# Layer 0's experts add their rows to the tokens in memory; layer 1's thresholds, casts and order of work change engines and places

## The chip, the cores and the metric

The kernel runs on one core of one Trainium2 chip, in one launch. The core has a matrix engine (TensorE, PE in the profile), a vector engine (VectorE, DVE), an engine for activations and copies (ScalarE, ACT), a general one (GpSimd, POOL) and one that only issues transfers (SyncE, SP). Each engine works through its own list of instructions in order; semaphores tie the lists together. Indirect transfers (gathers and scatters by a list of row numbers) are issued by POOL, plain ones mostly by SP. The metric is the time of the launch on the device in microseconds; 2173.75 is the median of three runs before the change.

## The reference

Two transformer layers work on 4096 tokens (2 sequences of 2048) of 256 numbers in float32. In both, attention and experts run beside each other on the normed tokens:

```
xn = layernorm(x)
x = x + attention0(xn) + experts0(xn)
xn = layernorm(x)
x = x + attention1(xn) + experts1(xn)
```

- `attention0`: causal attention with 16 heads, queries through a rank of 64, keys and values through a rank of 32, rotary positions, softmax.
- `experts0`: softmax over 8 experts, the best two per token; token and choice get a place in the expert's buffer while it has room (1280 places). An expert computes `(gelu(x Wa) * (x Wg)) Wout` with 512 hidden numbers. The two results of a token are weighed by its gates and summed.
- `attention1`: each token attends to 32 learned patterns per head by *sparsemax*: the 32 scores are sorted, summed up, and a threshold `tau` is found, so that `max(z - tau, 0)` sums to one.
- `experts1`: sigmoid scores, the best two of 8 experts per token; each expert's weight is the mean gate of its tokens; `down(silu(gate x) * (up x))` with 128 hidden numbers; and a shared expert with 256 hidden numbers for all tokens.

## The kernel before, in words

**Layer 0.** Attention fills the first 1200 us; a planner written by hand gives small jobs due times (`later("S", ISSUE, due, job)` puts a transfer on SP from a due time on). Its results, residual and attention, are stored to `x1` in memory (`store_sum`). The router and the dispatch run inside it: each normed token row is scattered to its expert's place in `buf` (line 654), with two more numbers, the row to which the result is to go and the gate (`ROW` is 258). `clear` (line 635) has filled `buf` beforehand; an empty place has 1e6 as the row to go to. `clear` also fills the result buffer `oe` of 2 x 4096 rows, by 16 transfers of 512 KB.

The experts follow (lines 1281 to 1296). An expert has 1152 places, in three steps of 384. Rows are turned by TensorE (L1252) and copied to `inT` by ScalarE and VectorE (L1254, L1256); for each of four parts of the hidden numbers TensorE makes `pa` and `pg` (L1265, two buffers each), ScalarE the gelu `ge` (L1267), VectorE the product `hT` (L1268); then TensorE makes `py` for three tiles of 128 rows (L1272), VectorE weighs them into `ys` (L1275) and POOL scatters `ys` to `oe` (L1276), choice 0 in the first half, choice 1 in the second, so that every row is written at most once. Rows with 1e6 are beyond `bounds_check` and are not written. Four views of `oe` that are declared disjoint (`out_ways`) let up to four scatters be under way. The numbers `to` and `gates` are cast and copied from the rows by VectorE (L1241, L1243), two buffers each.

**Layer 1.** Here all work is a list of tasks with an engine, a guessed duration, a lag, what they come after, and buffers (`Plan`, lines 49 to 127). `Plan.write` merges them: at each point it takes the earliest task, and on its engine, among those that could start about then, the one of the lowest rank (`RANKS`, line 1389, by function name), then the one with the longest way to the end. It thus writes one fixed order for each engine before anything runs; every instruction so written has line 138 in the profile.

- `prepare` (line 1446), for eight groups of 512 tokens: `add_results` (line 1425) loads the two `oe` halves and adds them to `x_sb` (which the expert loop has loaded from `x1`); mean and variance per tile (`bn_stats`, `bn_aggr`); `roots` makes the inverse root by 13 small instructions on VectorE; ScalarE norms into `xn`; TensorE turns (`tp`), ScalarE copies to `xT`, TensorE makes the router's logits (`po`), `bias_` adds on VectorE.
- `shared`: the shared expert's products (`gu`, `acc`). `router`: sigmoid, best two, counts, places. `dispatch`: 64 scatters of `xn` rows to `buf1`, from POOL.
- `routed`, 20 blocks of 512 places: POOL gathers the expert's weights from `wall`, SP loads the rows, VectorE casts the row numbers `to` (`places`), TensorE, ScalarE and VectorE compute, POOL scatters to `oe`.
- `sparsemax` (line 1775), 8 batches: VectorE and ScalarE sort by compares (tile `srt`), VectorE scans, finds `tau`; POOL subtracts it (`less`, `z<-z,tau`). `attend` and `project` use the result. All this needs only `xT`, and fills the time of dispatch and routed blocks.
- `combine` adds the two `oe` halves to `x_sb`; `store` writes the output.

Of the kernel before, what the change touches and what calls it, by code (L numbers as in the profile page):

```python
# [11 lines left out]
F32 = mybir.dt.float32  # L12
# [10 lines left out]
NT = B * S  # L23
# [25 lines left out]
class Plan:  # L49
# [3 lines left out]
    class Task:  # L53
        __slots__ = ("eng", "ns", "f", "after", "new", "lag", "nr", "rank", "way", "left", "ready", "next", "end", "at")
# [16 lines left out]
    def add(self, eng, ns, f, after=(), new=(), use=(), lag=0, rank=0):  # L71
        t = Plan.Task()
        t.eng, t.ns, t.f, t.after, t.new, t.lag, t.rank = eng, ns, f, list(after), list(new), lag, rank
        t.next, t.end, t.way = [], None, 0
        for h in list(new) + list(use):
            h.users.append(t)
        self.tasks.append(t)
        return t

    def write(self, until=0, slow=1):  # L80
# [27 lines left out]
        while ready:  # L108
# [4 lines left out]
            s, t = max((z for z in cand if z[1].eng == t0.eng and z[0] <= (soon if z[1].rank < t0.rank else s0 + near)), key=lambda z: (-z[1].rank, z[1].way))  # L113
# [32 lines left out]
def moe_transformer_kernel(  # L146
# [15 lines left out]
    x1 = dram.tile([NT, E], F32, name="x1")  # L162
# [111 lines left out]
    with ExitStack() as actx:  # L274
# [15 lines left out]
        zero = attw.tile([P, ROW], F32, name="zero")  # L290
# [30 lines left out]
        G.iota(number, pattern=[[NT, 2], [P, NTILE]], base=0, channel_multiplier=1)  # L321
# [235 lines left out]
        def store_sum(bq):  # L557
            sdma(x1.rearrange("(t p) d -> p t d", p=P)[:, 4 * bq:4 * bq + 4], xos[bq])
# [76 lines left out]
        def clear(b, i):  # L635
            n = b.shape[1]
            sdma(b[512 * i:512 * i + 512].rearrange("(p a) d -> p a d", a=4), bc(zero[:, 0:n], 1, [P, 4, n]))
# [501 lines left out]
        pin(G.memset(zero[:, E:ROW], 1e6))  # L1139
# [4 lines left out]
        later("S", 9 * ISSUE, 40000, load_out_weights, None, 2)  # L1144
        for i in range(NSLOT // 512):
            later("S", ISSUE, 50000 + 12000 * i, lambda i=i: clear(buf, i), None, 2)
            later("S", ISSUE, 340000 + 40000 * i, lambda i=i: clear(buf1, i), None, 2)
            if i < 2 * NT // 512:
                later("S", ISSUE, 360000 + 40000 * i, lambda i=i: clear(oe, i), None, 2)
# [78 lines left out]
    with tc.tile_pool(name="moe", bufs=2) as mp, tc.tile_pool(name="moeh", bufs=3) as hp, \  # L1228
            tc.tile_pool(name="moetp", bufs=2, space=PSUM) as mtp, \
            tc.tile_pool(name="moeps", bufs=2, space=PSUM) as mps:  # L1230
        out_ways = bass_types.dram_disjoint_views(oe[:], 4)
# [26 lines left out]
        def feed_forward(wi, wt, inT, n, to, gates_e, c0):  # L1258
# [10 lines left out]
            for i in range(n // P):  # L1269
                py = mps.tile([P, E], F32, tag="py", name="py")  # L1270
                for f in range(4):
# [4 lines left out]
                G.indirect_dma_start(out_ways[c % 4], bass.IndirectOffsetOnAxis(ap=to[:, c:c + 1], axis=0), ys, None,  # L1276
                                     bounds_check=2 * NT - 1, oob_is_err=False)
# [3 lines left out]
        for e in range(NE):  # L1281
# [10 lines left out]
            SP.dma_start(x_sb[:, 4 * e:4 * e + 4], x1.rearrange("(t p) d -> p t d", p=P)[:, 4 * e:4 * e + 4])  # L1292
# [22 lines left out]
    SP.dma_start(fg_sb, fg[:, :, NE:NE + 2])  # L1315
    SP.dma_start(fu_sb, fu[:, :, NE:NE + 2])
    SP.dma_start(fd_sb, fd[:, NE:NE + 2])
    xT = l1x.tile([P, 2, NT], F32, name="xT")
    scale = l1x.tile([P, NTILE, NE], F32, name="scale")
    with tc.tile_pool(name="l1a", bufs=2) as lp, \  # L1320
# [5 lines left out]
        NZ = 3  # L1326
        head = lc.tile([P, H1, NPAT], F32, name="head")
# [54 lines left out]
        for i in range(4):  # L1382
# [7 lines left out]
            "add_results.take": 8, "attend.flip": 3, "attend.keep_": -1, "attend.weigh": 3, "prepare.flip": -4,  # L1390
            "prepare.keep_": -3, "prepare.logits": -2, "routed.down": 1, "routed.fetch": 3, "routed.flip": -1,
            "routed.hidden": 1, "routed.keep_": 2, "routed.out_": 2, "routed.places": 4, "router.slots": 4,
            "router.totals": -2, "scores.go": 3, "scores.keep_": -2, "shared.<lambda>": -2, "shared.down": 3,
            "sparsemax.<lambda>": 4, "sparsemax.copy": -1, "sparsemax.divide": 4, "sparsemax.largest": 6,
            "sparsemax.less": 3, "sparsemax.threshold": 5
# [17 lines left out]
        def results(src, k, grp, dst):  # L1413
# [5 lines left out]
        land0 = [zbuf[1 + i // 2].rearrange("p h i s -> p (h i s)")[:, 1024 * (i % 2):1024 * (i % 2) + 1024].rearrange(  # L1419
            "p (c e) -> p c e", c=4) for i in range(4)]  # L1420
        land1 = [xn_flat[:, 1024 * i:1024 * i + 1024].rearrange("p (c e) -> p c e", c=4) for i in range(8)]
        r_land = plan.ring(4), plan.ring(8)
        turn_land = cycle(land0), cycle(land1)

        def add_results(src, which_, grp, after, xn4=None):
# [3 lines left out]
            for k in range(2):  # L1429
                hold, st = plan.hold(r_land[which_]), {}  # L1430
                direct = k == 0 and xn4 is not None

                def load(k=k, st=st, direct=direct):
                    st["at"] = xn4 if direct else next(turn_land[which_])
                    results(src, k, grp, st["at"])

                def take(st=st):
                    pV.tensor_tensor(xs, xs, st["at"], ALU.add)
                d = add("S", 1700, load, after, new=[] if direct else [hold], lag=3500)
                last = [add("V", 1220, take, [d] + last, use=[] if direct else [hold])]  # L1440
# [3 lines left out]
        normed, turned, logged, added = {}, {}, [], []  # L1444

        def prepare(grp):
            mv = lc.tile([P, 4, 2], F32, name=f"mv{grp}")
            sm = lc.tile([P, 4, 4], F32, name=f"sm{grp}")
            rstd, v, t, nmr = (sm[:, i] for i in range(4))
            xn4 = xn[:, 4 * grp:4 * grp + 4, 0:E]  # L1450
            stats = []
            added.extend(add_results(oe, 0, grp, [], xn4))
            for i in range(4):
# [571 lines left out]
```

## Time and profile before

| what | us |
|---|---|
| median of three runs (2168.76 to 2175.24) | 2173.75 |
| the profiled execution | 2170.47 |
| its span in the profile | 2168.7 |
| layer 0, attention with router and dispatch | 0 to about 1206 |
| layer 0, experts | about 1206 to 1603 |
| layer 1, first normed tokens to last logits | 1617 to 1687 |
| layer 1, first scatter of the dispatch | 1706.7 |
| layer 1, rows of the first routed block asked for | 1813.7 |
| layer 1, last threshold | 2119 |

The profile is of one execution. A group's line gives the line of code, engine, operation, what it writes and reads, shapes and count; then its busy time and the mean of one in ns; then the engine's idle time ahead of it and what ended most of that. A line of the timeline gives start, duration, engine, line and operation, and in brackets the idle time before it with the one that ended it. "PEld" is a weight load of TensorE. The granted clock is a share of TensorE's full clock. Over the whole span TensorE is busy 89%, VectorE 65%; from 1603 on it is 440 and 474 of 566 us.

### The profile page before, as it was taken

To read this page: it belongs to the slowest core of one execution; us is meant where nothing else is said; L and a number is where in the kernel's file an instruction comes from. 1 tells how busy PE (TensorE), PEld (TensorE's weight loads), DVE (VectorE), ACT (ScalarE), POOL (GpSimd) and SP (SyncE) were. 2 spreads that over 40 slices of the span, in tenths; PEclk is the share of its full clock that TensorE was granted. 3 is DMA by queue.
4 is the path that set the end of the run, shared out by engine and by line. 5 is a ranking of instruction groups with operands and counts; after the bars stand their busy time and mean duration, and the time that the engine had idled before them with its cause. 6 is when DMAs were issued, how large, how long until landed. Compare 5 with 4: busy or idle time off the path is not lost. (4 is left out here: it accounts for less than half of the span.)

```text
span 2168.7 us, 26456 instructions
## 1 busy us (share of the span) xinstructions
PE 1927.2 (89%) x9497; PEld 1074.1 (50%) x9510; DVE 1408.9 (65%) x2010; ACT 912.6 (42%) x1815; POOL 696.2 (32%) x920
## 2 busy tenths in 40 slices
PE   4689998999999999999998899999977985788886
PEld 2344443444444444444443566666746653566664
DVE  4476788677775678777771222222248797999875
ACT  3044455355566555655667111111114232554442
POOL 4232212343335234231001111111210486365652
PEclk8599899899999999999999899999995998999999
DMA  5433311442324333141100712221032123334427
GB/s 155 126 99 101 109 60 38 123 121 96 94 63 138 102 106 99 58 120 53 37 11 11 249 42 85 91 92 49 25 116 70 44 83 112 92 115 123 128 101 232
DMA packets 151064, 204.45 MB, mean 94 GB/s; under 512 B 16393, under 2 KB 116881, under 8 KB 150930
## 3 DMA queue, kind: packets, MB, share of 16 engines
q1 hardware_dynamic: 131264, 151.55, 23.1%
q0 software_dynamic: 16640, 49.41, 6.6%
q10 hardware_dynamic: 3026, 1.77, 0.3%
q8 instruction: 76, 1.25, 0.2%
q14 instruction: 58, 0.48, 0.1%
HBM read 109.13 MB, written 98.79 MB: 96 GB/s over the span
## 5 line engine op out<-in xcount | busy, mean ns | idle before, releaser
L509 ACT ACTIVATE es<-sc 128x512 f32<-128x512 f32 (+3 forms) x1280 | 599.5, 535 | 457.6 <-PE sc L309 443.7
L470 DVE TENSOR_REDUCE part<-s 128x2 f32<-128x1024 f32 (+3 forms) x640 | 650.1, 1058 | 207.2 <-PE s L309 206.1
L309 PE MATMUL sc<-q,ks 128*128 128x512 f32 (+3 forms) x1280 | 426.4, 419 | 19.9 <-ACT es L509 19.5
L309 PEld LDWEIGHTS sc<-q,ks 128*128 128x128 f32 x1280 | 212.5, 192 | 248.3 <-ACT es L509 173.7
L309 PE MATMUL av<-es,va 128*32 128x512 f32 (+3 forms) x2560 | 300.9, 548 | 3.7 <-POOL es L511 2.1
L309 PE MATMUL s<-ks,q 64*128 64x512 f32 (+3 forms) x1280 | 253.0, 447 | 32.8 <-DVE part L470 10.9
L511 POOL TENSOR_SCALAR_AFFINE_SELECT es<-es 128x256 f32<-128x256 f32 x256 | 103.3, 407 | 555.8 <-ACT es L509 554.8
L138 DVE TENSOR_TENSOR srt<-srt 128x1024 f32<-128x1024 f32 (+3 forms) x224 | 231.7, 1072 | 7.0 <-ACT srt L138 0.2
L309 PEld LDWEIGHTS s<-ks,q 64*128 64x128 f32 x1280 | 111.7, 189 | 199.3 <-DVE part L470 113.3
L1276 POOL DMA_INDIRECT oe<-ys,to x72 | 70.0, 972 | 335.1 <-DVE ys L1275 330.2
L1268 DVE TENSOR_TENSOR hT<-ge,pg 128x384 f32<-128x384 f32 x96 | 53.1, 554 | 185.9 <-PE pg L1265 184.7
L1267 ACT ACTIVATE ge<-pa 128x384 f32<-128x384 f32 x96 | 47.1, 490 | 269.2 <-PE pa L1265 269.1
L138 POOL DMA_INDIRECT oe<-xn,to x80 | 100.3, 1254 | 101.4 <-ACT xn L138 82.8
L138 POOL DMA_INDIRECT buf<-xn,slot x64 | 86.1, 1345 | 118.1 <-DVE rc L138 98.9
L1265 PE MATMUL pa<-inT,wi 128*128 128x384 f32 x336 | 123.3, 486 | 0.0
L1265 PE MATMUL pg<-inT,wi 128*128 128x384 f32 x336 | 122.1, 486 | 0.0
L138 ACT COPY srt<-srt 128x1024 f32<-128x1024 f32 (+2 forms) x80 | 66.7, 834 | 120.9 <-DVE srt L138 120.1
L1272 PE MATMUL py<-wt,hT 128*128 128x256 f32 x504 | 112.2, 379 | 0.0
L309 PEld LDWEIGHTS av<-es,va 128*32 128x32 f32 x2560 | 55.6, 109 | 99.7 <-issue 75.9
L1272 PEld LDWEIGHTS py<-wt,hT 128*128 128x128 f32 x504 | 95.8, 190 | 17.5
L1275 DVE TENSOR_SCALAR ys<-py,gates 128x256 f32<-128x256 f32 x72 | 34.8, 484 | 86.2 <-PE py L1272 86.2
L1265 PEld LDWEIGHTS pg<-inT,wi 128*128 128x128 f32 x336 | 63.3, 190 | 42.7
(262 smaller groups left out, 2349.4 us busy)
## 6 DMA issues: line engine op xcount, KB each, us to landing
q<-qd SPq DMA_DIRECT2D x64, 256.0 KB
xn<-oe SPq DMA_DIRECT2D x24, 512.0 KB
buf<-zero SPq DMA_DIRECT2D x20, 516.0 KB
buf<-zero SPq DMA_DIRECT2D x20, 514.0 KB
xn<-buf SPq DMA_DIRECT2D x20, 514.0 KB
rows<-buf SPq DMA_DIRECT2D x8, 1161.0 KB
qd<-hi SPq DMA_DIRECT2D x16, 512.0 KB
qd<-lo SPq DMA_DIRECT2D x16, 512.0 KB
```

The costliest lines, as they stand in the source:

```text
L138: return lambda *a, **k: self.tc.keep_in_program_order(f(*a, **k))
L309: pin(PE.matmul(*args, **kw))
L470: pin(V.tensor_reduce(parts[j][:, i, 2 * pair:2 * pair + 2, kb], sc[:, :, :n], AX.X, ALU.max))
L509: pin(A.activation(es[:, g % 2, :n], sc[:, :n], AF.Exp, scale=0.25))
L511: pin(G.affine_select(es[:, :, 0:P], es[:, :, 0:P], pattern=[[0, 2], [1, P]], compare_op=ALU.is_ge, fill=0.0, base=0, channel_multiplier=-1))
L1265: PE.matmul(ps[:, :n], lhsT=wi[:, dc, col:col + P], rhs=inT[:, dc], start=dc == 0, stop=dc == 1)
L1267: A.activation(ge[:, :n], pa[:, :n], AF.Gelu)
L1268: V.tensor_tensor(hT[:, f, :n], ge[:, :n], pg[:, :n], ALU.mult)
L1272: PE.matmul(py, lhsT=hT[:, f, P * i:P * i + P], rhs=wt[:, f], start=f == 0, stop=f == 3)
L1275: V.tensor_scalar(ys, py, gates_e[:, c:c + 1], None, ALU.mult)
L1276: G.indirect_dma_start(out_ways[c % 4], bass.IndirectOffsetOnAxis(ap=to[:, c:c + 1], axis=0), ys, None, bounds_check=2 * NT - 1, oob_is_er ...
```

## The change

1. Layer 0's experts scatter `ys` to `x1` itself, with an addition in the transfer (`compute_op=ALU.add`), without bounds check and without disjoint views, so that each such scatter waits for the one before it. `x1` has 128 rows more; an empty place now has row 4096 (`NT`), the first of these, as the row to go to. The row numbers lose the half of `oe` (`NT*k`); layer 1's `mark` adds it.
2. The 16 clears of `oe` go; one small store clears the spare rows of `x1`, one writes the first 128 rows of `oe`. The layout of a clear is `(a p)` in place of `(p a)`.
3. In layer 1 `x_sb` is loaded from `x1` by eight transfers in `measure`, after the last scatter; the 16 loads of `oe` halves and the 16 additions go. The shared expert's weights are loaded behind the first of the eight. `roots` works on groups 0, 1, 2-3, 4-5, 6-7: five batches in place of eight.
4. `warm`: 12 products of 128 x 512 on TensorE, whose result nobody reads, ahead of the first transposes.
5. `less` moves from POOL to VectorE, the cast `places` of the routed blocks from VectorE to ScalarE.
6. New `RANKS`; a key `sub` that breaks ties of rank (the loads in order of groups); the first compares of the two halves of a batch one after the other; `plan.write`'s factor on TensorE's guessed durations before 60 us is 1.15 and not 1.8. In the order so written, most of the shared expert's products stand behind the router.

The diff, cut to its core ("..." marks what is left out; the new `RANKS` are in the full kernel, and `roots` has the same instructions as before on wider slices):

```diff
-            s, t = max((z for z in cand if z[1].eng == t0.eng and z[0] <= (soon if z[1].rank < t0.rank else s0 + near)), key=lambda z: (-z[1].rank, z[1].way))
+            s, t = max((z for z in cand if z[1].eng == t0.eng and z[0] <= (soon if z[1].rank < t0.rank else s0 + near)), key=lambda z: (-z[1].rank, -z[1].sub, z[1].way))
...
-    x1 = dram.tile([NT, E], F32, name="x1")
+    x1 = dram.tile([NT + P, E], F32, name="x1")
...
-        zero = attw.tile([P, ROW], F32, name="zero")
+        zero = attw.tile([P, E + 1], F32, name="zero")
+        zero0 = attw.tile([P, ROW], F32, name="zero0")
...
-        G.iota(number, pattern=[[NT, 2], [P, NTILE]], base=0, channel_multiplier=1)
+        G.iota(number, pattern=[[0, 2], [P, NTILE]], base=0, channel_multiplier=1)
...
         def clear(b, i):
-            n = b.shape[1]
-            sdma(b[512 * i:512 * i + 512].rearrange("(p a) d -> p a d", a=4), bc(zero[:, 0:n], 1, [P, 4, n]))
+            z, n = (zero0, ROW) if b is buf else (zero, E + 1)
+            sdma(b[512 * i:512 * i + 512].rearrange("(a p) d -> p a d", a=4), bc(z, 1, [P, 4, n]))
...
-        pin(G.memset(zero[:, E:ROW], 1e6))
+        pin(G.memset(zero[:, E:E + 1], 1e6))
+        pin(G.memset(zero0, 0.0))
+        pin(G.tensor_scalar(zero0[:, E:E + 1], meta[:, 0, 0, 0:1], float(NT), None, ALU.add))
...
+        later("S", ISSUE, 48000, lambda: sdma(x1[NT:NT + P], zero0[:, 0:E]), None, 2)
+        later("S", ISSUE, 49000, lambda: sdma(oe[0:P], zero[:, 0:E]), None, 2)
         for i in range(NSLOT // 512):
             later("S", ISSUE, 50000 + 12000 * i, lambda i=i: clear(buf, i), None, 2)
             later("S", ISSUE, 340000 + 40000 * i, lambda i=i: clear(buf1, i), None, 2)
-            if i < 2 * NT // 512:
-                later("S", ISSUE, 360000 + 40000 * i, lambda i=i: clear(oe, i), None, 2)
...
-        out_ways = bass_types.dram_disjoint_views(oe[:], 4)
...
                 V.tensor_scalar(ys, py, gates_e[:, c:c + 1], None, ALU.mult)
-                G.indirect_dma_start(out_ways[c % 4], bass.IndirectOffsetOnAxis(ap=to[:, c:c + 1], axis=0), ys, None,
-                                     bounds_check=2 * NT - 1, oob_is_err=False)
+
+                G.indirect_dma_start(x1[:], bass.IndirectOffsetOnAxis(ap=to[:, c:c + 1], axis=0), ys, None,
+                                     compute_op=ALU.add)
...
-            SP.dma_start(x_sb[:, 4 * e:4 * e + 4], x1.rearrange("(t p) d -> p t d", p=P)[:, 4 * e:4 * e + 4])
...
-    SP.dma_start(fg_sb, fg[:, :, NE:NE + 2])
-    SP.dma_start(fu_sb, fu[:, :, NE:NE + 2])
-    SP.dma_start(fd_sb, fd[:, NE:NE + 2])
...
+        WARM = 12
...
+        def shared_weights():
+            pS.dma_start(fg_sb, fg[:, :, NE:NE + 2])
+            pS.dma_start(fu_sb, fu[:, :, NE:NE + 2])
+            pS.dma_start(fd_sb, fd[:, NE:NE + 2])
...
-            added.extend(add_results(oe, 0, grp, [], xn4))
...
-            roots_ = add("V", 2200, roots, stats)
...
+        def roots(g0, g1):
...
+        def measure(grp):
+            def load():
+                pS.dma_start(x_sb[:, 4 * grp:4 * grp + 4],
+                             x1[512 * grp:512 * grp + 512].rearrange("(c p) d -> p c d", p=P))
+            d = add("S", 1700, load, lag=3500, sub=2 * grp)
...
+        def warm():
+
+            hold, st, last = plan.hold(r_pz), {}, []
+
+            def product():
+                if not st:
+                    st["pz"] = psum("pz")
+                pPE.matmul(st["pz"], lhsT=ident, rhs=wo_sb.rearrange("p c e -> p (c e)"), start=True, stop=True)
+            for i in range(WARM):
+                last = [add("PE", 860, product, last, new=[] if i else [hold], use=[hold] if i else [])]
...
-                p = add("PE", 1750, lambda f=hidden: f(0), turned[blk] + ([] if e == 0 else [p]),
+                p = add("PE", 1750, lambda f=hidden: f(0), turned[blk] + weights + ([] if e == 0 else [p]),
...
-                pV.tensor_copy(xn[:, 8 * q:8 * q + 8, E], meta[:, k, 8 * q:8 * q + 8, 0])
+                pV.tensor_scalar(xn[:, 8 * q:8 * q + 8, E], meta[:, k, 8 * q:8 * q + 8, 0], float(NT * k), None, ALU.add)
...
-                pV.tensor_copy(st["to"], st["rows"][:, :, E])
+                pA.copy(st["to"], st["rows"][:, :, E])
...
-            i4 = add("V", 160, places, [r], new=[hto], use=[hr])
+            i4 = add("A", 300, places, [r], new=[hto], use=[hr])
...
-                pG.tensor_tensor(zr, zr, bc(tau["t"], 2, [P, n, NPAT]), ALU.subtract)
+                pV.tensor_tensor(zr, zr, bc(tau["t"], 2, [P, n, NPAT]), ALU.subtract)
...
-            done = [add("G", 200 + n * 58, less, [t] + sent)]
+            done = [add("V", n * 36, less, [t])]
...
-        for grp in range(NG):
-            prepare(grp)
+        warm()
+        for g0, g1 in ((0, 1), (1, 2), (2, 4), (4, 6), (6, 8)):
+            for grp in range(g0, g1):
+                measure(grp)
+                if grp == 0:
+                    weights.append(add("S", 2000, shared_weights, lag=3000, sub=0.5))
+            r = add("V", 2000, lambda f=roots, a=g0, b=g1: f(a, b), stats[4 * g0:4 * g1])
+            for grp in range(g0, g1):
+                rooted[grp] = r
...
-            sparsemax(b, c, flipped[order[n - NZ]] if n >= NZ else [placed["gates"]] if n == NZ - 1 else added if n else [])
+            sparsemax(b, c, flipped[order[n - NZ]] if n >= NZ else [placed["gates"]] if n == NZ - 1 else [])
...
-        plan.write(60000, 1.8)
+        plan.write(60000, 1.15)
```

## Prediction, made before the result was known

> **What bounds the kernel now.** I read the page's busy shares first, then the engines by stretch of layer 1, then the groups of VectorE (DVE), then one expert boundary of layer 0. Page:
>
> ```profile
> PE 1927.2 (89%) x9497; PEld 1074.1 (50%) x9510; DVE 1408.9 (65%) x2010; ACT 912.6 (42%) x1815; POOL 696.2 (32%) x920
> DMA  5433311442324333141100712221032123334427
> ```
>
> Up to 1603 us TensorE sets the pace (attention, then layer 0's experts); the transfers under attention fill a tenth to half of the DMA engines. Layer 1 is different. Its stretches (PE, weight loads, DVE, ACT, POOL busy; then clock, DMA share, GB/s):
>
> ```profile
> 1603.00:1617.00 14.00, 8.59 (x28) 4.51 (x28) 7.74 (x19) 2.16 (x4) 1.37 (x3) 1.00 0.60 188
> 1617.00:1677.00 60.00, 39.47 (x145) 30.24 (x146) 55.12 (x200) 23.65 (x44) 0.00 (x0) 0.56 0.34 111
> 1677.00:1706.00 29.00, 28.27 (x114) 18.14 (x113) 15.95 (x44) 9.31 (x15) 0.00 (x0) 0.98 0.00 1
> 1706.00:1815.00 109.00, 86.67 (x253) 51.31 (x255) 99.05 (x115) 28.62 (x42) 88.20 (x67) 0.95 0.23 81
> 1815.00:2119.00 304.00, 246.16 (x1115) 189.10 (x1125) 270.77 (x272) 141.65 (x228) 173.86 (x121) 0.92 0.36 113
> 2119.00:2169.00 50.00, 30.99 (x162) 20.77 (x160) 25.03 (x33) 8.92 (x17) 7.55 (x5) 0.94 0.77 252
> ```
>
> VectorE is about 90% busy from 1617 to 1677 and from 1706 to 2119; between 1677 and 1706 the router is a chain in which TensorE never rests. So a microsecond off VectorE in 1617–1677 is one off the end, and in 1706–2119 nearly one. Its groups (and one of POOL) in layer 1; columns are busy us, mean ns, idle before and who ended it:
>
> ```profile
> L138 DVE TENSOR_TENSOR x_sb<-x_sb,z 128x1024 f32<-128x1024 f32 x8 | 9.7, 1216 | 0.0
> L138 DVE TENSOR_REDUCE tau<-srt 128x64 f32<-128x2048 f32 x8 | 18.2, 2280 | 0.0
> L138 DVE CAST to<-xn 128x4 int32<-128x4 f32 x20 | 10.3, 517 | 10.7 <-DMA xn<-buf 10.7
> L138 DVE BATCH_NORM_STATS2 st<-x_sb 128x6 f32<-128x256 f32 x32 | 12.9, 402 | 0.2
> L138 DVE BATCH_NORM_AGGREGATE mv<-st 128x2 f32<-128x6 f32 x32 | 5.8, 182 | 1.1
> L138 POOL TENSOR_TENSOR z<-z,tau 128x2048 f32<-128x2048 f32 x8 | 31.1, 3885 | 7.1 <-DVE tau L138 5.6 <-ACT aT L138 1.4
> ```
>
> **Part 1: the scatters of layer 0's experts become a chain.** The last scatter of one expert and what follows, in order of time (start, duration):
>
> ```profile
> 1305.69 0.97 POOL L1276 DMA_INDIRECT oe<-ys,to  x1 [11.07 <-DVE ys L1275]
> 1309.15 0.97 POOL L1276 DMA_INDIRECT oe<-ys,to  x1 [0.76 <-DVE gates L1243]
> ...
> 1312.30 0.17 DVE L1241 CAST to<-rows 128x9 int32<-128x9 f32 x1 [0.36 <-DMA oe<-ys,to]
> 1313.47 0.55 DVE L1268 TENSOR_TENSOR hT<-ge,pg 128x384 f32<-128x384 f32 x1 [0.81 <-PE pg L1265]
> ```
>
> Over all 72 the time from issue to landing is
>
> ```profile
> DMA to landing us min/median/max: 2.0/2.4/5.9
> ```
>
> The cast of the expert after next reuses a `to` buffer, so it waits on VectorE for that scatter's landing: 1312.30−1309.15 = 3.15 us from start to landed. Today scatters go out 1.73 us apart and overlap. After the change each waits for the one before. A plain write would then cycle at c ≈ 3.2 us; [...]empty slots, today skipped, all add to one spare row. No row shows an accumulating scatter, so c is bounded: 3.2 below; above, 0.97 us of issue and the longest landing of these scatters, 5.9, is 6.9. [...] By the row alone c is 3.2[...]. I take 4.2, nearer the row[...].
>
> What c costs: a step takes about 16.5 us and issues three scatters, so up to c = 5.5 the chain keeps up. But at each expert boundary the cast stands ahead of the hT products on VectorE. TensorE has two product buffers and needs the first hT by about 1317.07 (the third pg of the expert). The cast starts at 1305.69+3c+0.2; with the small copy (0.28) and hT (0.55) behind it, TensorE stalls 3c−10.4 us. At six boundaries: c = 3.2: 0; c = 4.2: 2.2×6 = 13[...]. I take **+13 (0 to +40)**.
>
> **Part 2: no `oe` halves in layer 0.** The 16 clears of 512 KB lay under attention, at a DMA share of at most 0.5, so they are worth nothing[...].
>
> **Part 3: the start of layer 1.** Gone: 16 loads of 512 KB, 16 adds of 1.216 us = 19.5 us of VectorE, and three of eight batches of 13 small instructions near 0.165 us (some 2.5 us with gaps) = 7.5. New: the eight x loads stand on SP, and the first waits for the last scatter. Behind it are queued the three loads of shared weights and the other seven. The last three scatters start from 1599.3; 1599.3+3×4.2 = 1611.9, and about 5 us for issue and landing (the first `oe` load today needs 5.92 in the chain of waits) makes 1617, just when today's first add runs: moving the loads costs nothing more than that. POOL's small fills behind the last scatter slip 5 us, under the 99 us in which POOL waits before the dispatch.
>
> VectorE from 1617: 32×(0.402+0.182) = 18.7, five batches 12, eight biases 1.5: 32 us, to 1649. TensorE must keep up: a group is 8 transposes (1.80 us at full clock, in the chain of waits) and 16 logit products (1.69), so 8×3.5 = 28 us, behind a first lag of 6: 1651. At today's clock of 0.56 the rows give 64×0.287+128×0.224 = 47, so 1670. That is what the 12 unread products are for[...]. The products take 12×0.592 (a 128x512 product just before) = 7 us in today's gap before the first add, but then TensorE idles again for about 4 us until the first norm, [...]by the row (1.00 in 1603–1617) it is kept. I take 1656 against today's last bias at 1687.35: −31. In the router's chain up to 1706.7 some 9 us are gu and acc products of the shared block, which the new order puts mostly behind the router: −4 (0 to −8). **−35 (−17 to −45)**.
>
> **Part 4: thresholds and casts.** `less` moves from POOL to VectorE: 8×2.28 = +18.2 us, by the reduction of the same shape. Against it, VectorE is held while POOL runs `less`:
>
> ```profile
> 1824.51 4.49 POOL L138 TENSOR_TENSOR z<-z,tau 128x2048 f32<-128x2048 f32 x1 [1.44 <-ACT aT L138]
> 1825.54 6.79 DVE L138 TENSOR_TENSOR srt<-srt 128x1024 f32<-128x1024 f32 x3
> ```
>
> Three compares, 1.13 each elsewhere, took 6.79: 3.4 lost. The casts show it also (mean 517 ns where 160 is usual). Six or seven such holds are about −20. The casts on ScalarE: −3.2 of work, and a wait of 10.7 for rows leaves VectorE, of which I count half, since ScalarE then waits with sort copies and xg copies behind it that VectorE and TensorE need. 18.2−20−3.2−5 = **−10 (−22 to +6)**. In the tail the last `less` is 2.28 instead of 3.63 with its hand-over: **−2**.
>
> **Part 5: the new order.** 24 us of shared products (by stretch and tile: gu 7.1+11.4, acc 5.5 before 1706) move into 1706–2119. TensorE has 333 of 413 us busy there and gets 357 of about 400; VectorE is as full. [...]**+9 (0 to +24)**.
>
> **Sum** on the profiled run of 2170.5 (its span 2168.7): +13−35−10−2+9 = −25, so 2145. The median of the runs shown, 2173.75, lies 3 us above that run; differences below 0.3% (6.5 us) can't be told from none.
>
> **Rivals.** (a) *The chain of scatters becomes the bound.* Beyond c = 5.5 it is longer than TensorE's work: 72c from 1225.8. At c = 6 it ends at 1658, where my case has 1625 with its stall: 2145+33 = 2178; at 6.5, 2214. Break-even: −47+9 in the other parts against 6×(3c−10.4), c = 5.6. For it: [...]landings up to 5.9 us; against: a median landing of 2.4. I put it at 2195. (b) *The start's gain is eaten.* The clock stays at half (1670), ScalarE's waits return the cast gain and all 24 us of moved products show: +14+5+15 on my case: 2179 at the very worst, more likely half, 2162. For it: clock 0.56 now; against: fewer VectorE pauses between the groups. (c) *Everything packs.* c near 3.5, clock full, no give-back: −13−5−9: about 2118. For it: the 3.15 us row.
>
> **Chances.** My case 0.54 (2128 to 2160), (c) 0.12, (b) 0.14 with about a third of it within 0.3% of before, (a) 0.20 with a little of it at break-even. Faster 0.76, same 0.05, slower 0.19. The range leaves out the far half of (a) and of (c): 2112 to 2194.
>
> **What would show it.** Part 1: starts of neighbouring scatters 4.2 us apart, `to` casts waiting about 7 us, TensorE idle 2 us at six boundaries, clock still 1.00. Part 3: no adds before the bn_stats, last bias 31 us sooner after the experts' end, a clock above 0.8 there. Part 4: compares of 1.13 without holds, the row wait on ScalarE. Part 5: VectorE's share in the routed stage not below 0.88. Wrong if scatters are over 5.5 us apart, or the dispatch starts less than 10 us sooner.

## The result, and the profile after

The changed kernel takes 2156.3 us (median of 11 runs, 2148.3 to 2165.2) against 2175.2 for the kernel before (11 runs, 2168.8 to 2181.1): a ratio of 0.9916, with a 95% interval of 0.9895 to 0.9937. It is about 19 us faster. Ratios and their intervals leave out runs more than 1.5% above the fastest of their kernel; medians and ranges take in all runs. The profiled execution took 2153.0 against 2170.5, 17.5 less; the forecast for it was 2145, 25 less. Its page, the span and the busy shares:

```profile
span 2151.3 us, 26273 instructions
PE 1930.9 (90%) x9534; PEld 1072.2 (50%) x9534; DVE 1385.6 (64%) x1943; ACT 915.0 (43%) x1835; POOL 722.8 (34%) x914
```

The stretches of layer 1 after (columns as before: PE, weight loads, DVE, ACT, POOL busy; clock, DMA share, GB/s), from the first `x` rows to the last bias, to the first scatter of the dispatch, to the first rows of the routed blocks, nearly to the last threshold (2104.8), and to the end:

```profile
1637.00:1697.00 60.00, 53.59 (x232) 39.86 (x231) 35.34 (x161) 28.76 (x53) 0.66 (x2) 0.74 0.26 84
1697.00:1716.50 19.50, 18.29 (x51) 10.21 (x50) 14.95 (x40) 4.57 (x7) 0.00 (x1) 1.00 0.00 0
1716.50:1822.00 105.50, 97.35 (x318) 59.45 (x318) 101.95 (x113) 33.39 (x52) 85.69 (x66) 1.00 0.23 81
1822.00:2100.00 278.00, 226.75 (x1050) 174.57 (x1051) 258.29 (x255) 137.86 (x237) 160.85 (x115) 0.93 0.39 125
2100.00:2151.00 51.00, 32.48 (x172) 21.95 (x171) 34.59 (x38) 10.18 (x18) 7.51 (x4) 0.98 0.75 247
```

Before, VectorE was the busy one in the first stretch (55 of 60 us); now it is TensorE (54 of 60), at a clock of 0.74. The time went as follows, by points that both traces have, beside what the prediction's sum gave each:

| from, to | before | after | difference | forecast |
|---|---|---|---|---|
| start to first work on `x_sb` (add, then bn_stats) | 1617.2 | 1641.3 | +24.1 | +13 |
| to the last bias of the logits | 69.9 | 55.6 | -14.3 | -31 |
| to the first scatter of the dispatch | 19.6 | 19.6 | 0.0 | -4 |
| to the end of the last `less` | 416.1 | 392.9 | -23.2 | -3 |
| to the end of the span | 45.9 | 41.9 | -4.0 | 0 |
| sum | 2168.7 | 2151.3 | -17.4 | -25 |

(The forecast of -3 is -10-2+9, parts 4 and 5 of the prediction.) So the total was near the forecast, with errors of 10 to 20 us in both directions: the scatters cost nearly twice what was thought, the start of layer 1 gained half, and the routed stage gained 20 us more than was forecast.

A correction to what was said of the kernel: an empty place does not have row 4096. The fill is 4096 plus the token number of the first tile, so the rows to go to are 4096 to 4223, one for each row of a tile. No spare row is written twice by one scatter; the one spare row to which, by the prediction's part 1, all empty slots add does not exist.

**The boundary of two experts**, the place of the prediction's part 1, in the timeline after (start, duration):

```profile
1310.30 1.55 POOL L1279 DMA_INDIRECT x<-ys,to  x1 [5.16 <-DVE ys L1277]
1314.97 1.55 POOL L1279 DMA_INDIRECT x<-ys,to  x1 [3.13 <-DVE inT L1258]
1319.58 1.55 POOL L1279 DMA_INDIRECT x<-ys,to  x1 [3.06 <-DMA x<-ys,to]
1323.83 0.17 DVE L1243 CAST to<-rows 128x9 int32<-128x9 f32 x1 [6.83 <-DMA x<-ys,to]
1323.94 1.02 DVE L1270 TENSOR_TENSOR hT<-ge,pg 128x384 f32<-128x384 f32 x2
1324.55 1.56 PE L1267 MATMUL pg<-inT,wi 128*128 128x384 f32 x4 [2.71 <-DVE hT L1270]
```

The scatters are 4.6 us apart, the cast stands 6.83 us on VectorE, two `hT` products come out together behind it, and TensorE starts the third `pg` 2.71 us late: the forecast chain, link by link. In the view of waits from 1210 to 1640 us (us in total, times, longest), and in the landings of all 72 scatters, it reads

```profile
PE pg L1267 <- DVE hT L1270: 17.0, 6, 3.5
DVE to L1243 <- DMA x<-ys,to: 41.8, 6, 7.6
DMA to landing us min/median/max: 3.6/3.8/4.7
```

where landings took 2.0/2.4/5.9 before. From one expert's first scatter to the next one's took 48.9 us before; now 53.5, 51.9, 54.4, 54.0, 52.3, 51.1 and 48.9: six boundaries with 23.8 us together. Of these, 17.0 are the stalls, and 5.9 are longer `pa` and `pg` products (126.8 and 124.5 us against 123.3 and 122.1). Behind three of the six stalls, of 2.66, 3.10 and 3.52 us, the granted clock was half for some 3 us (0.50 from 1273 to 1275, 1378 to 1381 and 1433 to 1435); behind the other three (2.71, 3.10 and 1.93) it stayed at 1.00. Behind the one of 3.52, which ended at 1377.3:

```profile
1378.00:1380.00 2.00, 2.00 (x4) 1.01 (x3) 0.25 (x1) 0.00 (x0) 0.00 (x0) 0.50 0.00 0
```

The last three scatters, 4.5 apart, add 5.5 us to the end of the chain. The first work on `x_sb` hardly feels them: VectorE's own work ahead of it ends at 1641.05, also 23.8 later than before, and the first `bn_stats` starts at 1641.27.

### The profile page after: what moved, and what is told of

Its sections match the earlier page's. It is cut to its first block, busy times and chain, and to the rows that moved or that the text cites. A ratio compares the mean times of both kernels' runs of the same rounds, so it can differ in the third digit from the quotient of the medians.

```text
span 2151.3 us, 26273 instructions
## 1 busy us (share of the span) xinstructions
PE 1930.9 (90%) x9534; PEld 1072.2 (50%) x9534; DVE 1385.6 (64%) x1943; ACT 915.0 (43%) x1835; POOL 722.8 (34%) x914
## 3 DMA queue, kind: packets, MB, share of 16 engines
q1 hardware_dynamic: 114656, 135.03, 20.9%
## 5 line engine op out<-in xcount | busy, mean ns | idle before, releaser
L310 PE MATMUL sc<-q,ks 128*128 128x512 f32 (+3 forms) x1280 | 426.2, 419 | 19.6 <-ACT es L510 19.4
L138 DVE TENSOR_TENSOR srt<-srt 128x1024 f32<-128x1024 f32 (+3 forms) x224 | 223.2, 1034 | 7.6 <-DVE srt L138 0.5
L1279 POOL DMA_INDIRECT x<-ys,to x72 | 111.5, 1549 | 323.4 <-DVE ys L1277 178.6
L1267 PE MATMUL pg<-inT,wi 128*128 128x384 f32 x336 | 124.5, 493 | 17.0 <-DVE hT L1270 17.0
L138 POOL DMA_INDIRECT oe<-xn,to x80 | 114.9, 1437 | 63.6 <-ACT xn L138 44.4
L1267 PE MATMUL pa<-inT,wi 128*128 128x384 f32 x336 | 126.8, 498 | 0.0
L310 PEld LDWEIGHTS av<-es,va 128*32 128x32 f32 x2560 | 55.6, 109 | 99.9 <-issue 75.7
L1274 PEld LDWEIGHTS py<-wt,hT 128*128 128x128 f32 x504 | 95.8, 190 | 17.5
```

The source lines that it names most:

```text
L138: return lambda *a, **k: self.tc.keep_in_program_order(f(*a, **k))
L310: pin(PE.matmul(*args, **kw))
L1267: PE.matmul(ps[:, :n], lhsT=wi[:, dc, col:col + P], rhs=inT[:, dc], start=dc == 0, stop=dc == 1)
L1274: PE.matmul(py, lhsT=hT[:, f, P * i:P * i + P], rhs=wt[:, f], start=f == 0, stop=f == 3)
L1279: G.indirect_dma_start(x1[:], bass.IndirectOffsetOnAxis(ap=to[:, c:c + 1], axis=0), ys, None, compute_op=ALU.add)
```

## The experiments

The runs were made on three chips, each with its own runs of the kernel before. On the first were: eight buffers, the chain without the addition, no unread products, the old order; on the second: unread products between the groups, `less` on POOL again, the casts, the changed kernel once more; on the third: `less` alone on VectorE, the shared products after the dispatch, eight buffers again. "Changed" is the kernel after the change.

**Eight buffers for the row numbers (twice).** If the chain of scatters costs time only through the cast, more buffers for `to` must take the stalls away.

```diff
-            to = mp.tile([P, m], I32, tag="to", name="to")
+            to = mp.tile([P, m], I32, tag="to", bufs=NE, name="to")
```

> The changed kernel with eight buffers in place of two for layer 0's row numbers (to), so that no cast waits for the landing of a scatter. Theory A (the chain costs time only through the wait of the cast on VectorE, and where it runs on behind the last expert): the five to six stalls of TensorE vanish, the last scatter starts near 1608 us and not 1632 (TensorE's own work ends at 1602.5, and the last two scatters add 2 x 4.5 where they were 2 x 1.73 apart), the whole is about 24 us faster than the changed kernel: some 2132, ratio to before 0.981. Rival B (the chain of additions itself is the bound, or slows the expert stage through memory): scatters 4.5 us apart leave gaps only through that chain, so the stage stays near 1632 and the time near 2156.

> The changed kernel with eight row-number buffers in layer 0 once more, for its time: in its profile the expert stage was 23.5 us shorter than the changed kernel's, but the stretch from dispatch to first threshold 31 us longer. Theory A (that delay comes and goes, the shorter stage stays): over more runs it is 15 to 25 us faster than the changed kernel's median of the same chip (2156 to 2170): ratio to before 0.980 to 0.987. Rival B (what is won in layer 0 is lost in the dispatch in most executions): ratio 0.990 or more.

Measured on the first chip: 2151.3 us (four runs, 2137.8 to 2162.0), ratio 0.9877 (0.9793 to 0.9961); on the third: 2134.2, ratio 0.9801 (0.9778 to 0.9824), five runs within 6.5 us. In both profiles the stage is what theory A said: from expert to expert 48.9 us seven times, no stall of TensorE on `hT`, the last scatters at (third chip)

```profile
1599.46 1.55 POOL L1279 DMA_INDIRECT x<-ys,to  x1 [4.98 <-DVE ys L1277]
1603.88 1.54 POOL L1279 DMA_INDIRECT x<-ys,to  x1 [2.87 <-DVEq L1299]
1608.37 1.55 POOL L1279 DMA_INDIRECT x<-ys,to  x1 [2.94 <-DMA x<-ys,to]
```

1608.4 in place of 1632.1. The scatters are as slow as ever (4.4 and 4.5 us apart), and cost TensorE nothing. On the third chip this version is 2% faster than the kernel before. It never ran in one set with the changed kernel, whose ratios were 0.9916 and (below) 0.9944. On the first chip the 23.5 us won in layer 0 were lost again between the dispatch and the first threshold (85.8 us instead of 55.0; more on that below); on the third this stretch took 55.0, and 17.1 us of the gain stayed (span 2134.2 against 2151.3), the thresholds taking 6.5 us more from first to last.

**The same chain without the addition.** The scatters overwrite rows of `x1` and still wait for each other, so the experts' sums are left out. What follows in layer 1 works on other numbers, and only the expert stage is compared.

```diff
-                G.indirect_dma_start(x1[:], ..., ys, None,
-                                     compute_op=ALU.add)
+                G.indirect_dma_start(x1[:], ..., ys, None)
```

> The changed kernel without the addition in layer 0's scatters: they overwrite rows of x1 (the sums of experts and residual are left out), and each still waits for the one before. Theory A (the addition is dear[...]): issue on POOL 0.97 us and neighbours 3.2 to 3.3 us apart in place of 1.55 and 4.5; stalls of TensorE at the boundaries gone (3x3.2 is below 10.4), last scatter near 1606, about 2132 us. Rival B (the order is dear, or the missing bounds check, not the addition): issue stays 1.55 and distance 4.5, and the time stays near 2156.

One run, 2155.0 us. Theory A is right on the price of the addition: issue 0.96 us (1.55 with it; 0.97 in the kernel before, with its bounds check) and 3.16 us from start to start (4.51). So the addition costs 0.59 us on POOL and 0.76 in landing and hand-over. But the stalls did not go, as both it and the prediction's formula 3c-10.4 said they would: TensorE stood 9.2 us for `hT`, the six boundaries took 12.6 us more than before, and the last scatter started at 1620.6, not 1606. Where the time goes is seen in the timeline of one boundary:

```profile
1362.39 0.96 POOL L1279 DMA_INDIRECT x<-ys,to  x1 [2.73 <-DVE gates L1245]
1366.18 0.96 POOL L1279 DMA_INDIRECT x<-ys,to  x1 [2.83 <-DMA x<-ys,to]
1371.54 0.17 DVE L1243 CAST to<-rows 128x9 int32<-128x9 f32 x1 [6.15 <-DMA x<-ys,to]
```

The second scatter takes 3.8 us to the third, and the third 5.4 to the cast, where most neighbours elsewhere are 3.15 apart. At the six boundaries it is 11.8 to 12.9 us from the first of the last three scatters to the cast, where three times 3.16 is 9.5. SP issues the next weights and rows (1 MB, 0.5 MB and 1.16 MB) at the boundary, and the last scatters of an expert run beside them (here `wt` is issued at 1361.38 and `rows` at 1365.10). The changed kernel shows little of it: 12.8 to 14.3 us at its six boundaries, where three times 4.51 is 13.5. Of the 23.8 us, then, about half (12.6) stays without the addition. That the loads slow the plain chain is my reading of these times of issue and was not shown: no run moved them.

**No unread products.**

```diff
-        warm()
```

> The changed kernel without the 12 unread products. Theory A (the clock was lost again before the transposes could use it, so they bring little): within 3 us of the changed kernel, 2154 to 2160, clock in the 60 us after the first x load at most 0.05 lower than 0.74. Rival B (they keep the clock up in the start of layer 1): clock 0.56 as before the change, last bias some 8 us later, time 2162 to 2166.

The last bias came at 1696.6 us against 1696.9, and the dispatch began at 1716.2 against 1716.5: theory A for the stage, though the mean clock of 60 us there was 0.63, further below 0.74 than it allowed. The time, a median of 2180.7 (20 runs, 2153.4 to 2194.3; ratio 0.9975, 0.9944 to 1.0006), fits neither: in the profile the stretch after the dispatch is long again, 87.2 us. What became of the clock is seen in the changed kernel in stretches of 4 us:

```profile
1646.00:1650.00 4.00, 1.94 (x8) 0.75 (x7) 3.55 (x18) 2.07 (x4) 0.00 (x0) 1.00 1.10 352
1650.00:1654.00 4.00, 1.44 (x9) 1.11 (x8) 3.52 (x19) 2.33 (x5) 0.00 (x0) 0.62 0.86 272
1654.00:1658.00 4.00, 4.00 (x20) 4.00 (x21) 2.17 (x10) 1.29 (x3) 0.00 (x0) 0.50 0.02 6
...
1666.00:1670.00 4.00, 3.00 (x25) 2.64 (x23) 3.54 (x18) 3.67 (x7) 0.00 (x0) 1.00 0.00 0
1670.00:1674.00 4.00, 3.20 (x16) 2.82 (x16) 3.56 (x18) 4.00 (x9) 0.00 (x0) 0.68 0.01 2
1674.00:1678.00 4.00, 4.00 (x20) 3.78 (x21) 2.00 (x12) 2.97 (x7) 0.00 (x0) 0.50 0.00 0
1678.00:1682.00 4.00, 4.00 (x21) 3.74 (x19) 0.00 (x0) 3.31 (x7) 0.00 (x0) 0.50 0.02 4
...
1694.00:1698.00 4.00, 4.00 (x22) 3.08 (x21) 1.29 (x3) 0.42 (x1) 0.00 (x0) 1.00 0.00 0
```

The unread products run from 1636.1 to 1646.6 and end with a clock of 1.00. TensorE then has 3.4 us of work in 8: the first group's transposes, up to 1650.4, still run at full clock, 14 of its logit products, from 1653.4 to 1656.5, at half (3.16 us). The products of the shared expert (128x512) run from 1658.1 to 1661.4; the 16 logit products behind them take 1.85 us, at a clock of 1.00. The clock falls again near 1671.5, at the end of 4 us of which TensorE was busy for only 2.2. Then it stays at half while TensorE is 100% busy, from 1672 on, with transposes and logit products of 8 columns; the next shared products run from 1687.6 to 1691.4, and the clock is 1.00 behind them.

**Unread products between the groups.** On top of the eight buffers, two more products of 128x512 ahead of each group's transposes from the second on.

```diff
+        FILL = 2
...
+            for i in range(FILL):
+                last = [add("PE", 430, product, last, ...)]
...
-                p = add("PE", 1000, flip, n4, new=[hold])
+                p = add("PE", 1000, flip, n4 + (filler(grp) if grp and dc == 0 else []), new=[hold])
```

> Eight row-number buffers in layer 0, and two more unread products of 128x512 ahead of each group's transposes from the second on. Theory A (in the start of layer 1 the clock falls to half because transposes and logit products of 8 columns, though they fill TensorE, do not keep it up, and TensorE is the bound there): granted clock above 0.9 from the first group to the last bias, the 16 logit products 1.7 us in every group and not 3.2, and the last bias at most 46 us after the first bn_stats, where it is 56 in the changed kernel; the whole 30 to 35 us faster than the changed kernel if no other stretch changes. Rival B (VectorE or ScalarE bounds the start, or the products only add their own 14 us): last bias 55 us or more after the first bn_stats.

Rival B. Six of eight groups of logits took 1.85 to 1.95 us, as at full clock; in the first group 14 products took 3.16, in the seventh 16 took 3.58, both in stretches of 6 us with a clock of 0.50. But the last bias came 68 us after the first bn_stats (55.6 in the changed kernel): the products stand in TensorE's own chain, and with the waits for ScalarE in each group (0.7 us) they cost more than they brought. 2161.4 us, ratio to before 0.9927 (0.9891 to 0.9963), with 81.7 us from dispatch to first threshold.

**The old order.** The old table of ranks, and 1.8 for TensorE's guessed durations.

> The changed kernel with the old table of ranks and the old factor 1.8 on TensorE's guessed durations. Theory A (the 27 us that layer 1 gained from the first dispatch to the end, where 3 were forecast, come from the new order): most is lost, 2172 to 2184. Rival B (they come from less on VectorE and casts on ScalarE, which take away waits whatever the order): at most 8 us are lost, 2156 to 2164.

2204.3 us, ratio 1.0121 (1.0046 to 1.0197): even more than theory A had. Some 27 us of it lie before the dispatch (last bias at 1723.9, where the changed kernel has 1696.9), and from first to last threshold it takes 345.1 us, near the 351.2 before; the changed kernel and the variants that keep its order of this stage take 325 to 333, and 340 with eight buffers on the third chip. The old ranks were written for other tasks, so this prices an order that doesn't fit, not the old order in the old kernel.

**`less` on POOL again, and `less` alone on VectorE.** First in the changed kernel, with all other engines' orders left; then in the kernel before.

```diff
-                pV.tensor_tensor(zr, zr, bc(tau["t"], 2, [P, n, NPAT]), ALU.subtract)
+                pG.tensor_tensor(zr, zr, bc(tau["t"], 2, [P, n, NPAT]), ALU.subtract)
```

> The changed kernel with less emitted on POOL again, every other engine's order untouched. Theory A (moving less to VectorE costs 18 us of work there, and takes away holds of VectorE of about 20 and waits of TensorE for POOL): within 8 us of the changed kernel, either way; single compares and additions of 3 to 4 us come back on VectorE beside each less. Rival B (the waits for POOL are the gain: the first less stands behind the 64 scatters of the dispatch, TensorE's transposes wait 15 us for it): 12 to 25 us slower than the changed kernel, most of it lost between the first two thresholds.

> The kernel before with less alone emitted on VectorE, all orders else as they were. Theory A (less on VectorE is worth the 26 us between the first and the last threshold that its return to POOL cost in the changed kernel, 351.0 against 325.4): first to last threshold 325 to 335 us in place of 351.2, and 15 to 25 us faster than before: 2150 to 2160. Rival B (its worth hangs on the new order): 343 us or more from first to last threshold, time within 8 us of before.

In the new order the return to POOL costs 21 us by the medians (2190.8 against 2169.9 for the changed kernel on the same chip; ratios 1.0081, 1.0048 to 1.0114, and 0.9944). The waits for `less`, in the tile's view (duration in ns, first and last start) and among TensorE's waits from 1779 to 1850 us:

```profile
L138 POOL TENSOR_TENSOR z<-z,tau x8: 3636/3657/4483, 1810.6 to 2135.1; 128x2048 f32<-128x2048 f32 x8
PE tp L138 <- POOL z L138: 22.9, 1, 22.9
```

The threshold is there at 1779.5 + 2.3, but `less` starts at 1810.6, behind the last scatters of the dispatch, and TensorE's next transposes stand 22.9 us. From first to last threshold it took 351.0 us, where the changed kernel's profile on this chip has 325.4, and 22 of the difference lie between the first two. But that other profile had its first threshold 21 us later after the dispatch, by the delay told below, so the second threshold stands 134 to 135 us behind the dispatch in both (102.5 in the first profile of the changed kernel). How much of the 21 us this wait makes is not settled by the two profiles.

In the old kernel, `less` on VectorE brings nothing: 2177.7 us, ratio 1.0002 (0.9985 to 1.0019), thresholds 357.7 us from first to last. The old order asks for `less` only after the scatters are sent, and so its first one starts at 1809.7 on VectorE, 41 us behind its threshold. There the prediction's balance holds: the work is 18.3 us, the compares get shorter (1086 to 1033 ns on 168 of them, 8.9 us), the casts lose their holds (none over 0.41 us, where their mean was 0.517), and VectorE's wait for the rows grows from 10.7 to 17.1 us. Rival B for the old order, then; that the move is worth something in an order that asks for the first `less` while the scatters still run fits the 22.9 us and the medians.

**The casts on VectorE again.**

```diff
-                pA.copy(st["to"], st["rows"][:, :, E])
+                pV.tensor_copy(st["to"], st["rows"][:, :, E])
```

> The changed kernel with the casts of the routed blocks' row numbers on VectorE again, at the same places of the written order. Theory A (the wait of 15 us for the first rows on ScalarE holds less behind it than it would on VectorE): 5 to 12 us slower than the changed kernel, VectorE waiting 8 to 15 us for xn<-buf. Rival B (the wait moved and nothing was gained, since VectorE waits 9.9 us for the cast on ScalarE anyway): within 3 us.

Rival B: ratio 0.9948 (0.9920 to 0.9977), beside 0.9944 for the changed kernel on the same chip (medians 2174.3 and 2169.9); first to last threshold 325.4 in both. In the first profile of the changed kernel ScalarE waits 14.8 us for the rows, and a product `h` on VectorE 9.9 us for ScalarE's cast. Neither profile of this pair has such a wait: both carry the delay told next, and the rows were there before the cast.

**The changed kernel once more.**

> The changed kernel once more, for the spread of its own stages. Theory A (the 30 us by which the first threshold came later after the dispatch's start in the runs without unread products and with eight row-number buffers belong to those kernels): dispatch start to first threshold 55 us as in its first profile, and times of 2148 to 2165. Rival B (these delays come and go from one execution to the next in any of these kernels): this stretch differs from 55 us by more than 10 in this profile, or the times spread by over 20 us.

Rival B. 20 runs from 2146.8 to 2191.5, median 2169.9, ratio 0.9944 (0.9918 to 0.9971), where the first 11 runs lay within 17 us. In its profile the last bias came sooner, 49.8 us after the first `bn_stats` in place of 55.6. Its third and fourth bias are 4.06 us apart (1670.22 and 1674.28), as in the first profile (1671.84 and 1675.90), where the 16 logit products between them took 3.42 us at a clock of 0.50. But by 1678 the clock was back (the first line, a stretch of 2 us; the next 16 took 1.85 us), behind transposes and logit products alone and before the next shared products at 1681.9:

```profile
1676.00:1678.00 2.00, 2.00 (x16) 1.74 (x14) 0.00 (x0) 2.00 (x6) 0.00 (x0) 0.76 0.04 8
1677.29 1.85 PE L138 MATMUL po<-gw_sb,xT 128*128 128x8 f32 x16
1681.91 1.96 PE L138 MATMUL gu<-xT,fg_sb 128*128 128x512 f32 x4
```

So one program met both clocks in one stretch of its work; what decides between them is open. But after the dispatch (first line: this execution; second: the first profile of the changed kernel; both from the first dispatch scatter to the first threshold)

```profile
1708.70:1795.30 86.60, 54.78 (x157) 33.56 (x161) 52.77 (x68) 16.14 (x25) 64.59 (x57) 0.82 0.24 86
```

```profile
1716.50:1771.50 55.00, 54.57 (x164) 33.48 (x165) 52.46 (x68) 16.40 (x26) 44.33 (x36) 1.00 0.24 84
```

the same work of TensorE, VectorE and ScalarE, in 31.6 us more. By the end of the launch 23.6 of them are left (458.4 us from the first scatter of the dispatch on, against 434.8). VectorE's waits in this execution:

```profile
1728.13 0.69 DVE L138 TENSOR_TENSOR hs<-si,gu 128x512 f32<-128x512 f32 x1 [4.63 <-remote]
1757.06 1.22 DVE L138 TENSOR_TENSOR x_sb<-x_sb,acc 128x1024 f32<-128x1024 f32 x1 [23.04 <-remote]
1766.08 0.69 DVE L138 TENSOR_TENSOR hs<-si,gu 128x512 f32<-128x512 f32 x1 [3.72 <-ACT si L138]
```

The `acc` products that the second one reads are in TensorE's record by 1731; it starts 26 us later ("remote": the trace knows no releaser), and TensorE itself stands 30 us, to 1766. POOL's scatters run on at 1.28 us until 1760, with one gap of 7.0 us behind that. In seven profiles on the first two chips, all with the new order, this stretch took 65 to 87 us; on the third, with the same order, 55.0, and with the old order (before, the old ranks, `less` alone) 56 to 59.

**The shared expert's products after the dispatch.** To see whether that delay needs those products beside the scatters; with the eight buffers.

```diff
-        for blk in range(NG):
-            shared(blk)
         router()
...
+        weights.extend(sent)
+        for blk in range(NG):
+            shared(blk)
```

> Eight row-number buffers, and the shared expert's products held back until all 64 scatters of the dispatch are sent. The changed kernel and its variants took either 55 us from the dispatch's first scatter to the first threshold (one profile) or 65 to 87 (seven profiles), with VectorE, ScalarE and TensorE waiting for each other's results up to 23 us. Theory A (the delays need the tight exchange of the shared expert's products among the three engines, with one or two buffers each, beside the scatters): this stretch falls to 60 us or less, no wait of VectorE over 3 us in it, and the times of one kernel spread by less than 15 us. Rival B (the delays come from the scatters or from elsewhere, whatever TensorE does): waits of 4 us and more and a spread over 25 us remain.

From the dispatch to the first threshold it took 47.5 us, no wait of VectorE in it was over 1.3, and the times of four runs spread by 12 us, as theory A has it. But on the same chip the kernel with eight buffers showed no delay either, so the run decides nothing. It costs dear: 2217.2 us, ratio 1.0175 (1.0140 to 1.0209), since VectorE then waits 43.5 us for `gu`, most of it behind the last threshold, from which it takes 119.2 us to the end (46.5 in the changed kernel). What causes the delay is open: it was not tried, for instance, with other buffers in that exchange.

## Why the prediction was right, and where it was not

**The sum and its sign** were right, 25 us forecast and 17.4 found in the profiled executions, by errors of up to 20 us in both directions that cancelled. That the total came near is in part luck.

**Part 1, the chain.** The mechanism was right: the chain hides behind TensorE, except through the cast ahead of `hT`. Taking away the buffer's wait took away all of it. The term that was mis-sized is c, 4.2 assumed and 4.51 measured: with it the formula gives 3.1 us a boundary, 19 us together, and 17.0 were measured. The issue on POOL grew (1.55 for 0.97), which no bound of mine contained, and the landing grew from 2.4 to 3.8. The row alone (3.2) is what a plain chain does, 3.16; the step from there to 4.2 was an estimate of mine. The addition puts 1.35 us on top, 0.59 of issue and 0.76 of landing and hand-over; what either consists of, no run shows. Another 6 us, the slower products, were put at nothing: "clock still 1.00" did not hold behind three of the six stalls. +24 in place of +13.

**Part 2** was right as far as the trace can tell: nothing in layer 0 up to the experts moved (first scatter of the experts at 1225.8 in both).

**Part 3, the start.** VectorE's part was right (34 us from the first bn_stats to the last norm's numbers, forecast 32; no adds), and so was the case that was set against mine: the "1670" that the half clock gives is 53 us after the first work, 55.6 were measured. The step that failed is "I take 1656". The 12 products took 10.6 us and not 7 (each is two records of 128x512), so that TensorE idled for 1.6 us ahead of the first transposes and not 4. Their effect lasted for these alone (1.00, 0.62, 0.50 in the stretches from 1646 to 1658), and leaving them out changed the stage by 0.3 us. That the clock is kept, which I had read from the row of 1603 to 1617, did not hold: it fell in the stretch of 8 us, 1646 to 1654, in which TensorE had 3.4 us of work. Later TensorE was full from 1672 on, and the clock stayed at 0.50 for 18 us. Of the 15.2 us from 1672.4 to 1687.6, 5.4 went to transposes and 9.8 to logit products of 8 columns; in the second execution the clock came back while the same two ran (0.76 in 1676 to 1678). What takes the clock away and what brings it back, no run shows. The 4 us for the router did not come either: the chain from last bias to dispatch is 19.6 us in both, with other products in it.

**Part 4** had the right balance for the old order (forecast about 0 for `less`, found 1.0002), but the move of the casts, put at some -8 us (3.2 of work and half of a wait), came out at nothing (0.9948 with them on VectorE, 0.9944 without). The sum left out a wait of the kernel before, that of TensorE for POOL's first `less`:

```profile
PE tp L138 <- POOL z L138: 15.2, 1, 15.2
```

In the changed kernel it is gone, and with `less` on POOL it was 22.9 us.

**Part 5** probably had the wrong sign: parts 4 and 5 together were put at -3 and came to -23. From the dispatch to the last `less`, before and after:

```profile
1706.70:2122.80 416.10, 334.93 (x1383) 242.03 (x1395) 369.26 (x384) 173.01 (x276) 265.65 (x188) 0.93 0.32 104
```

```profile
1716.50:2109.40 392.90, 330.12 (x1411) 238.50 (x1411) 369.54 (x372) 176.83 (x298) 252.19 (x183) 0.95 0.34 110
```

VectorE is busy 369 us in both; its idle time fell from 46.8 to 23.4. So the 18 us of `less` that came in are balanced by holds and casts that went (224 compares at 1034 ns in place of 1072, 8.5 us; 16 first compares, 1.7; the casts, 10.3), and the whole gain is idle time that went. The order and the moved `less` took it out together; no run parts them cleanly. The +9 for two engines at 90% was an estimate of mine that no run bears out: VectorE reached 94% (369.5 of 392.9 us).

**Rivals.** (a) the chain never became the bound: 4.5 is below 15.5/3 = 5.2 (a step within an expert is 15.5 us; the 16.5 that I wrote is near the mean with the boundary, 48.9/3 = 16.3). (b) held for the clock. (c) held for the packing. The delay after the dispatch was in none of them, and is as large as any: on the chip where it was seen in the changed kernel, the lead over the kernel before was 0.6% by the ratio and 0.2% by the medians of all runs.

## What to carry to other kernels

When transfers are chained, ask first which instruction waits for the end of the chain, and on which engine; here one cast with two buffers turned a hidden chain into 24 us, and more buffers for 4.6 KB a piece took them back (0.980 of the time before, on one chip). Price a moved instruction in the order in which it will stand: `less` was worth nothing in one order and, by the medians, 21 us in the other. And profile a kernel more than once when its times spread: the first trace of the changed kernel shows nothing of the delay of 31.6 us that the second has.

## What had not been expected of the hardware

- A scatter of 128 rows of 1 KB with addition: 1.55 us of POOL and 4.51 from start to start when chained; without it 0.96 and 3.16.
- TensorE 100% busy with 128x128 transposes and products of 8 columns stayed at a granted clock of 0.50 for 18 us (1672 to 1690) in one execution, until products of 128x512 had run; in another execution of the same program it was back by 1678 (0.76 in 1676 to 1678; the 16 logit products from 1677.3 took 1.85 us), before the next such products at 1681.9.
- An addition on VectorE that started 26 us after the record of the products that it reads (1731 to 1757 in the changed kernel's second profile, VectorE idle for 23.0 of it); in five other profiles it waited 4.1 to 20.9 us so. Seen on two of three chips, and only with the new order; unexplained.
